# A two-layer gated network on one NeuronCore: a first layer in TensorE order written out by hand, side work in tables of slots, and every half of W2 multiplied from a split

## The chip, the cores and the metric

The program runs on one core of one Trainium2 chip. Its time is device time in microseconds (us), from the launch of the program to its end on that core. The kernel before was timed three times; the figure compared is the median. One further execution was taken with the hardware profiler.

## The reference

The input x has 4 batches of 512 tokens with 256 features, all in float32. The hidden width is 1024. Both layers have the same shape, `x = x + mix(xn) * silu(ffn(xn))` with `xn = layernorm(x)`; they differ in `mix`. Cut to what is computed:

```python
def ffn(x, W1, W3, W2):                      # W1, W3: 1024 x 256, W2: 256 x 1024
    hidden = silu(x @ W1.T) * (x @ W3.T)
    hidden = fwht(hidden)                    # Walsh-Hadamard over 1024, / sqrt(1024)
    return hidden @ W2.T

def mix0(x):                                 # one step of a recurrence from a zero state
    xi = (x @ W_in.T)                        # 512 channels, 16 states each
    y = sum(C_real * B_real * xi - C_imag * B_imag * xi, over the states)
    return x + rmsnorm(y @ W_out.T) * norm_w

def mix1(x):                                 # causal attention with one head of 256
    n = layernorm(x) * gamma + beta
    q, k, v = n @ qkv[:, :256], n @ qkv[:, 256:512], n @ qkv[:, 512:]
    return softmax(causal(q @ k.T / 16)) @ v @ o_proj + x

for mix, W1, W3, W2 in layers:
    xn = layernorm(x)
    x = x + mix(xn) * silu(ffn(xn, W1, W3, W2))
```

## The kernel before

**Precision.** A float32 operand is split into a part `hi`, a cast to the format fp32r that TensorE reads, and `lo = src - hi`. `split` does this with a cast on ACT (line 61) and a subtraction on DVE (line 62). `mm3` (line 80) then makes one product out of three of TensorE: hi by hi, lo by hi and hi by lo, added up in one PSUM bank. All TensorE instructions go through one helper, so that all have line 70 in the profile; they are told apart by their tiles.

**Weights.** The Walsh-Hadamard transform is moved from the hidden values to W2: `prep_w2` takes each half of W2 (128 of the 256 outputs, `w2raw`, 512 KB) through three butterfly stages on DVE (lines 155 and 156, tiles `w2b`) and then through a product with a 128 by 128 Hadamard matrix on TensorE (tile `w2ps`, two of 512 columns for a half), and splits the outcome into `w2h` and `w2l`. For half 0 of layer 0 that product is native: TensorE reads float32 on both sides (line 170). The other three halves are split first (`w2bh`, `w2bl`) and take two fp32r products for each 512 columns. `prep_m` folds W_in, the coefficients and W_out into one matrix m of 256 by 256 (tile `mps`). `prep_second` forms the products of the query and key weights and of the value and output weights, and `prep_s` forms sums of layer 1's weights, splits them and stores them to DRAM.

**First layer.** `ffn` works on one batch of 512 tokens in 8 chunks of 128 hidden features. A chunk has the gate and the up product (`gu`, three PSUM banks, 6 fp32r products of 512 columns for each of the two), silu on ACT (line 526, tile `h`), the gate product on DVE (line 527), the split of `h` into `hh` and `hl`, and the down products (`dn`, 12 of 256 columns). The down products of a chunk are issued `defer` = 1 chunks later, those of batch 0 all at the end. The trace calls the tiles of a batch f_0gu, f_1h and so on, and leaves the number of the layer or of the batch out where it can't tell them apart.

**Side work.** Beside the chunks go the mixer (`mixer`: 24 products of 256 columns, a copy `osb` and squares on ACT, a power on POOL, a scaling and an addition into `xn` on DVE, lines 730 and 733), the gate of the batch before (`gate`: silu on ACT, lines 702 and 704 on DVE, which give the new `x`), the layernorm and the transposes of the next batch (`norm`: statistics and scaling on DVE, a power on POOL, eight transposes on TensorE into the tiles `xt..tp0` and `tp1`, which are split into `xt`), and the preparation of weights. They are generators. The class `Beside` runs through them one after the other and spreads their steps evenly over 16 slots for each batch, two for each chunk: `slot(2 * c)` ahead of a down chunk and `slot(2 * c + 1)` behind it. Small PSUM results share three banks with the tag `ms`; the down products have two.

**Order of the engines.** Each engine's instructions are put in order when the program is built: the tile framework's scheduler places an instruction by its own model of time, as soon as that model says that its operands are there, and `issue_after` forces one instruction behind another. Queues are then worked through in order on the chip. `line["fixed"]` puts each TensorE instruction behind the one issued before it in the program; it is set at the end of layer 0, so that in layer 0 the scheduler chooses TensorE's order and in layer 1 the program does. DMAs go out from the SP queue, save half of the first load of x, which goes from ACT.

**Second layer.** `ffn_s` does the gate and up products with seven block products instead of eight, the attention's steps stand in tables (`places`) between them, and the order of TensorE is the program's.

Of the kernel before, what the change touches and what calls it, by code (L numbers as in the profile page):

```python
# [21 lines left out]
P = 128  # L22
D = 256
# [12 lines left out]
def kernel(ctx: ExitStack, tc: tile.TileContext, a: dict, out: bass.AP):  # L36
# [22 lines left out]
    def split(src, hi, lo, engine=nc.vector):  # L59

        h = nc.scalar.copy(hi, src)  # L61
        return h, engine.tensor_tensor(lo, src, hi.bitcast(F32), ALU.subtract)  # L62

# [13 lines left out]

    def mm3(o, terms, late=False):  # L80


        seq = [(l[0], r[0]) for l, r in terms]
        if late:
            seq += [(l[1], r[0]) for l, r in terms] + [(l[0], r[1]) for l, r in terms]
        else:
            for l, r in terms:
                seq += [(l[0], r[1]), (l[1], r[0])]
        for n, (l, r) in enumerate(seq):
            ins = matmul(o, l, r, start=n == 0, stop=n == len(seq) - 1)  # L90
        return ins
# [30 lines left out]
    def split_w13(layer, q, raw):  # L122
        both = wp.tile([P, 2, 2, S], F32R, tag="w13", name=f"w13_{layer}_{q}", bufs=4)
        hi, lo = both[:, 0], both[:, 1]
        if (layer, q) != (0, 0):
            split(raw, hi, lo)
            return hi, lo
        halves = [slice(c * D, (c + 1) * D) for c in range(2)]
        split(*(z[:, :, halves[0]] for z in (raw, hi, lo)))
        next(normed)  # L130
        with after(first["norm"][0]), after(first["norm"][1]):
            hi_, lo_ = split(*(z[:, :, halves[1]] for z in (raw, hi, lo)))
        first["w13"] = hi_, lo_
        return hi, lo
# [7 lines left out]

    def prep_w2(layer, raws, dst, scratch):

        w2h, w2l = dst
        for half in range(2):
            ds_ = slice(half * P, (half + 1) * P)
            cur = raws[half]  # L150
            for st, h in enumerate((1, 2, 4)):
                nxt = scratch(f"w2b{st}_{layer}_{half}", [P, NH, P])
                cv = cur.rearrange("p (g two h) d -> p g two (h d)", two=2, h=h)
                nv = nxt.rearrange("p (g two h) d -> p g two (h d)", two=2, h=h)
                nc.vector.tensor_tensor(nv[:, :, 0], cv[:, :, 0], cv[:, :, 1], ALU.add)
                nc.vector.tensor_tensor(nv[:, :, 1], cv[:, :, 0], cv[:, :, 1], ALU.subtract)
                cur = nxt
                yield

            native = layer == 0 and half == 0  # L160
            if not native:
                bh = t4(f"w2bh_{layer}_{half}", [P, NH, P], F32R)
                bl = t4(f"w2bl_{layer}_{half}", [P, NH, P], F32R)
                split(cur, bh, bl)
                yield
            for q in range(2):
                o = psum(f"w2ps_{layer}_{half}_{q}", [P, NH // 2, P])
                qs = slice(q * NH // 2, (q + 1) * NH // 2)
                if native:
                    matmul(o, had_f, cur[:, qs, :], start=True, stop=True)  # L170
                else:
                    matmul(o, had, bh[:, qs, :], start=True, stop=False)
                    matmul(o, had, bl[:, qs, :], start=False, stop=True)
                split(o, w2h[:, qs, ds_], w2l[:, qs, ds_])
                yield
# [14 lines left out]

    def prep_m(win, wout):

# [6 lines left out]
        wg = [t4(f"wg{i}", [P, 4, D], F32R) for i in "hl"]  # L199
        wi = [t4(f"wi{i}", [P, 4, D], F32R) for i in "hl"]  # L200
        for c in range(4):
# [4 lines left out]
            )  # L206
        split(win, *wi)
        yield
# [255 lines left out]

    def ffn(name, xT, w13, w2, slot, defer=1, spare=(), parts=1, behind=False, tail=()):

# [33 lines left out]
        for c in range(NH):  # L500
# [8 lines left out]
            for half in range(parts if c == 0 else 1):  # L509
                n = S // (parts if c == 0 else 1)  # L510
                ts_ = slice(half * n, (half + 1) * n)
                if parts == 1 or c:
                    for o, cols in gu:
                        last_up = mm3(o[:, ts_], k_pairs((wh, wl), cols, xT, ts_))
                    continue

                for n, (w, x) in enumerate(((wh, xT[0]), (wl, xT[0]), (wh, xT[1]))):
                    for o, cols in gu:
                        for k in range(2):
                            last_up = matmul(  # L520
                                o[:, ts_], w[:, k, cols], x[:, k, ts_],
                                start=n + k == 0, stop=n + k == 3,
                            )
            gu = [o for o, _ in gu]
            h = hid(f"{name}h{c}")
            first["silu"] = nc.scalar.activation(h, gu[0], AF.Silu)
            gates.append(nc.vector.tensor_tensor(h, h, gu[1], ALU.mult))  # L527
            first["gate"] = gates[-1]
# [184 lines left out]
    def mixer(b):  # L713
# [5 lines left out]
        for i in range(2):  # L719
            o = psum(f"o0_{b}_{i}", [P, 2, D])  # L720
            for j in range(2):
                mm3(o[:, j, :], k_pairs(xT, sl(2 * i + j), m, ALLD))
            nc.scalar.copy(osb[:, 2 * i : 2 * i + 2, :], o)
# [12 lines left out]
    class Attention:  # L736
# [45 lines left out]
        def tq(self, j):  # L782
# [3 lines left out]
            o = psum(f"tq{b}_{j}", [P, S])  # L786
            mm3(o, k_pairs(first["wqk"], sl(j), self.xg, ALLS), late=self.b > 0)
            split(o, self.tqs[0][:, j, :], self.tqs[1][:, j, :])
# [92 lines left out]
    class Beside:  # L881


        def __init__(self, *tasks, slots=2 * NH):
            self.slots = slots
            self.gens = [g for g, _ in tasks]
            self.total = sum(n for _, n in tasks)
            self.done = 0

        def step(self):  # L890
            while self.gens:
                try:
                    next(self.gens[0])
                    self.done += 1
                    return True
                except StopIteration:
                    self.gens.pop(0)
            return False

        def slot(self, k):  # L900
            if k + 1 >= self.slots:
                self.finish()
            while self.done < self.total * (k + 1) / self.slots and self.step():
                pass

        def finish(self):
            while self.step():
                pass

# [3 lines left out]
    def call(f, *args):  # L913
        f(*args)
        yield


    NORM, MIXER, W2P = 3, 3, 12

# [42 lines left out]
    def prep_first():  # L962
# [3 lines left out]
        yield  # L966
        for _ in range(4):
# [12 lines left out]
        next(product)  # L980
# [7 lines left out]
    def prep_second():  # L988
# [9 lines left out]
        yield  # L998


    dn = None
    for b in range(B):
        tasks = []
        if b == 0:
            prep = prep_first()
            next(prep)
            tasks.append((prep, 12))
        if b:
            tasks.append((call(gate_all, f"g0_{b - 1}", dn, xns[0, b - 1], xs[b - 1]), 1))
        tasks.append((mixer(b), MIXER))  # L1010
        if b + 1 < B:
            if b:
                load_x(b + 1)
            if b == 2:
                tasks.append((prep_s(0), 4))
            tasks.append((norm(0, b + 1), NORM))
        if b == 0:
            early = w2_tile("early0"), w2_tile("early1")
            spare = [
                [early[i][:, 2 * c : 2 * c + 2, :].rearrange("p a d -> p (a d)") for i in range(2)]  # L1020
                for c in range(NH // 2)
            ]
        if b == 1:
            raw2_1 = load_w2(1)
            w2_1 = w2_tiles(1)
            tasks.append((prep_w2(1, raw2_1, w2_1, t4), W2P))
            tasks.append((prep_second(), 5))
        if b == 2:
            tasks += [(prep_s(1), 4), (norm(1, 0), NORM), (prep_s(2), 4)]
        if b == 3:  # L1030
            atts = [Attention(0)]
            at = atts[0]
            parts = run(at.xt_half, 0), run(at.xt_half, 1), at.xt, at.scaled, at.split_sums
            tasks += [(call(f), 1) for f in parts]
            norms = {1: norm(1, 1)}
            tasks.append((prep_s(3), 4))
        bg = Beside(*tasks)
        if b == 0:
            dn = ffn("f0_0", xTs[0, 0], w13, w2, bg.slot, NH, spare, parts=2, behind=True)
        else:  # L1040
            tail = [run(atts[0].tq, j) for j in range(2)] if b + 1 == B else []
            dn = ffn(f"f0_{b}", xTs[0, b], w13, w2, bg.slot, tail=tail)
        bg.finish()

# [28 lines left out]

    line["fixed"] = True
    gate_all("g0_3", dn, xns[0, 3], xs[3])
    behind = None
    for b in range(B):
# [15 lines left out]
        if not final:  # L1093
            if b == 0:
                next(norms[1])
            places[0][2].append(run(next, norms[b + 1]))
# [95 lines left out]
```

## Time and profile before

| | us |
|---|---|
| median of 3 runs | 359.23 (359.09 to 359.24) |
| the profiled execution | 359.27 |
| its span in the profile | 357.5 |
| TensorE matmuls (PE) busy | 351.5 |
| weight loads (PEld) busy | 327.4 |
| VectorE (DVE) busy | 287.1 |
| ScalarE (ACT) busy | 197.6 |
| GpSimd (POOL) busy | 20.8 |

The span is the time from the first to the last instruction that the profiler saw; the 1.8 us between it and the execution's time lie around it. Busy times are sums over an engine's instructions; matmuls are pipelined, so that the busy time of one holds a part of the next. The clock that was granted to TensorE was 1.00. The DMA engines moved 52.25 MB, a mean of 146 GB/s. In the rows of a timeline the first column is the start, the second the duration of the group, then come the engine, the line, the operation, the tile written, the tiles read, the shapes and the count; in square brackets stand the idle time of the engine before the group and what ended it.

### The profile page before, as it was taken

Reading aid. Unit: us, or ns where it says so; the run is one execution under the profiler, and the core shown is the slowest. Engines: PE = TensorE matmul, PEld = TensorE weight load, DVE = VectorE, ACT = ScalarE, POOL = GpSimd, SP = SyncE. Lnnn points to the kernel's source line nnn. Section 1 sums busy time; section 2 is a strip of 40 time slices with the busy share of each in tenths; the row PEclk is TensorE's granted clock in tenths of the full one; section 3 lists DMA queues with packets and bytes.
Section 4 is the critical chain, followed back from the end, with each engine's and each line's share of the span. In section 5 each row is a group of like instructions: output and inputs, shape, how many; then the busy total and the mean of one; then the engine's idle time right before and its main releaser. Section 6 shows DMA issues by size and latency. Waiting matters only on the chain.

```text
span 357.5 us, 6272 instructions
## 1 busy us (share of the span) xinstructions
PE 351.5 (98%) x2477; PEld 327.4 (92%) x2477; DVE 287.1 (80%) x597; ACT 197.6 (55%) x373; POOL 20.8 (6%) x22
## 2 busy tenths in 40 slices
PE   8999999999999999999999999999999999999995
PEld 6878998888988898888999999999999999999995
DVE  6899648998579938898887957989679897568645
ACT  3666156256373424674367655576555676556443
POOL 2000110300020210100110001100011000000000
PEclk9999999999999999999999999999999999999999
DMA  7935000301044416656357145562554745345401
GB/s 222 357 95 202 2 1 2 92 25 61 0 151 160 163 27 219 256 177 198 129 208 254 27 191 207 205 224 105 205 193 150 230 169 205 142 150 192 194 2 59
DMA packets 16284, 52.25 MB, mean 146 GB/s; under 512 B 1632, under 2 KB 7936, under 8 KB 16256
## 3 DMA queue, kind: packets, MB, share of 16 engines
q1 hardware_dynamic: 15968, 51.60, 41.0%
q8 instruction: 19, 0.31, 0.4%
q10 hardware_dynamic: 288, 0.26, 0.2%
q14 instruction: 9, 0.07, 0.1%
HBM read 42.40 MB, written 9.45 MB: 145 GB/s over the span
## 4 chain that ended last, share of the span: by engine, by line
PE 98%; DVE 1%; ACT 0%; issue 0%; DVEq 0%
PE f_1dn L70 6%; PE f_2dn L70 6%; PE f_1gu L70 6%; PE f_0dn L70 6%; PE f_0gu L70 6%; PE f_2gu L70 6%; PE f_3gu L70 6%; PE f_3dn L70 6%; PE sc L70 4%; PE pv L70 4%; PE o L70 3%; PE v L70 3%; PE tq L70 3%; PE warm L70 2%; PE w2ps L70 1%; PE pt L70 1%
## 5 line engine op out<-in xcount | busy, mean ns | idle before, releaser
L70 PE MATMUL f_1gu<-xt,w 128*128 128x512 f32 x96 | 24.9, 396 | 0.3 <-ACT xt L61 0.3
L70 PE MATMUL f_3gu<-xt,w 128*128 128x512 f32 x96 | 25.0, 396 | 0.0
L70 PE MATMUL f_2gu<-xt,w 128*128 128x512 f32 x96 | 24.8, 395 | 0.0
L70 PE MATMUL f_0gu<-xt,w 128*128 128x512 f32 (+1 forms) x108 | 24.4, 379 | 0.0
L70 PEld LDWEIGHTS f_0gu<-xt,w 128*128 128x128 f32 x108 | 18.5, 188 | 4.5 <-issue 1.0
L70 PEld LDWEIGHTS f_1gu<-xt,w 128*128 128x128 f32 x96 | 17.0, 188 | 3.6 <-ACT xt L61 0.5
L70 PEld LDWEIGHTS f_2gu<-xt,w 128*128 128x128 f32 x96 | 17.0, 188 | 3.0
L70 PEld LDWEIGHTS f_3gu<-xt,w 128*128 128x128 f32 x96 | 17.0, 188 | 2.9
L61 ACT CAST f_2hh<-f_2h 128x512 fp32r<-128x512 f32 x16 | 10.0, 622 | 15.3 <-DVE f_2h L527 12.2
L70 PE MATMUL f_3dn<-w2l,f_3hh 128*128 128x256 f32 x64 | 17.7, 281 | 0.0
L70 PE MATMUL f_1dn<-w2l,f_1hh 128*128 128x256 f32 x64 | 17.7, 281 | 0.0
L70 PE MATMUL f_3dn<-w2h,f_3hh 128*128 128x256 f32 x64 | 17.7, 281 | 0.0
L70 PE MATMUL f_2dn<-w2h,f_2hh 128*128 128x256 f32 x64 | 17.7, 282 | 0.0
L70 PE MATMUL f_1dn<-w2h,f_1hh 128*128 128x256 f32 x64 | 17.6, 280 | 0.0
L70 PE MATMUL f_2dn<-w2l,f_2hh 128*128 128x256 f32 x64 | 17.6, 280 | 0.0
L70 PE MATMUL f_3dn<-w2h,f_3hl 128*128 128x256 f32 x64 | 17.0, 281 | 0.0
L70 PE MATMUL f_1dn<-w2h,f_1hl 128*128 128x256 f32 x64 | 17.0, 281 | 0.0
L70 PE MATMUL f_2dn<-w2h,f_2hl 128*128 128x256 f32 x64 | 16.7, 281 | 0.0
L61 ACT CAST f_3hh<-f_3h 128x512 fp32r<-128x512 f32 (+1 forms) x17 | 10.0, 594 | 10.2 <-DVE f_3h L527 6.0
L61 ACT CAST f_1hh<-f_1h 128x512 fp32r<-128x512 f32 x16 | 9.9, 622 | 9.7 <-DVE f_1h L527 6.6
L62 DVE TENSOR_TENSOR f_2hl<-f_2h,f_2hh 128x512 fp32r<-128x512 f32 x16 | 11.0, 686 | 4.5 <-ACT f_2hh L61 4.5
L62 DVE TENSOR_TENSOR f_3hl<-f_3h,f_3hh 128x512 fp32r<-128x512 f32 (+1 forms) x17 | 11.1, 655 | 3.7 <-ACT f_3hh L61 3.6
(487 smaller groups left out, 1149.0 us busy)
## 6 DMA issues: line engine op xcount, KB each, us to landing
sw<-s SPq DMA_DIRECT2D x32, 896.0 KB, 5.3
s<-sp SPq DMA_DIRECT2D x8, 512.0 KB, 4.6
s<-sp SPq DMA_DIRECT2D x8, 384.0 KB, 2.8
w2raw<-in_w SPq DMA_DIRECT2D x4, 512.0 KB, 5.4
sraw<-in_w SPq DMA_DIRECT2D x4, 512.0 KB, 3.3
mrb<-there SPq DMA_DIRECT2D x4, 512.0 KB, 3.7
w13raw<-in_w SPq DMA_DIRECT2D x3, 512.0 KB, 6.8
x<-in_x SPq DMA_DIRECT2D x3, 512.0 KB, 3.6
```

Of the source, the lines that this page charges most:

```text
L61: h = nc.scalar.copy(hi, src)
L62: return h, engine.tensor_tensor(lo, src, hi.bitcast(F32), ALU.subtract)
L70: ins = call(*args, **kwargs)
```

## The change

Six things are done at once.

1. **W2 all from splits.** Half 0 of layer 0 is split like the others and takes two fp32r products for each 512 columns; the native product is gone. `prep_w2` takes the halves that it is to do, so that the two halves of layer 1 become two generators.
2. **A split by DMA.** `split_by_dma` has ACT write the negated source to `lo` and the cast to `hi`, and has a DMA of the POOL queue add the source to `lo`. It is used for `w13_0_3`, the last quarter of layer 0's gate and up weights, behind the silu of chunk 2, and for `win`.
3. **Order in `mm3`.** The lo parts of one side come together, those of the left or of the right side last (`late`), instead of in turn.
4. **Down products two chunks later.** `defer` becomes 2, and the last down chunk of a batch is handed on (`pend`) and issued behind chunk 0 of the next batch's gate and up products.
5. **A fixed order.** `line["fixed"]` is set from batch 1 of layer 0 on.
6. **A table of slots.** `Beside` stays for batch 0 alone and takes a list of steps there. Batches 1 to 3 have a list of 16 slots each, with the steps of each slot written out. The gate has two steps now (silu, then the rest).

```diff
+    def split_by_dma(src, hi, lo):
+        nc.scalar.mul(lo, src, -1.0)
+        nc.scalar.copy(hi, src)
+        nc.gpsimd.dma_start(lo.bitcast(F32), src, accum_op=ALU.add)
...
-    def mm3(o, terms, late=False):
+    def mm3(o, terms, late=0):
         seq = [(l[0], r[0]) for l, r in terms]
-        if late:
-            seq += [(l[1], r[0]) for l, r in terms] + [(l[0], r[1]) for l, r in terms]
-        else:
-            for l, r in terms:
-                seq += [(l[0], r[1]), (l[1], r[0])]
+        for side in (1 - late, late):
+            seq += [(l[1 - side], r[side]) for l, r in terms]
...
-        if (layer, q) != (0, 0):
-            split(raw, hi, lo)
+        if q:
+            with after(first["silus"][2] if q == 3 else None):
+                (split_by_dma if q == 3 else split)(raw, hi, lo)
             return hi, lo
...
-            native = layer == 0 and half == 0
-            if not native:
-                bh = t4(f"w2bh_{layer}_{half}", [P, NH, P], F32R)
-                bl = t4(f"w2bl_{layer}_{half}", [P, NH, P], F32R)
-                split(cur, bh, bl)
-                yield
+            bh, bl = (t4(f"w2b{i}_{layer}_{half}", [P, NH, P], F32R) for i in "hl")
+            split(cur, bh, bl)
+            yield
...
-                if native:
-                    matmul(o, had_f, cur[:, qs, :], start=True, stop=True)
-                else:
-                    matmul(o, had, bh[:, qs, :], start=True, stop=False)
-                    matmul(o, had, bl[:, qs, :], start=False, stop=True)
+                matmul(o, had, bh[:, qs, :], start=True, stop=False)
+                matmul(o, had, bl[:, qs, :], start=False, stop=True)
...
-    def ffn(name, xT, w13, w2, slot, defer=1, spare=(), parts=1, behind=False, tail=()):
+    def ffn(name, xT, w13, w2, slot, defer=2, spare=(), parts=1, behind=False, tail=(), pend=()):
...
+            if c == 0:
+                for what in pend:
+                    what()
...
-        line["fixed"] = bool(tail)
-        line["last"] = last_up
+        left = [lambda q=q: down(*q) for q in queue]
+        if not behind:
+            left.pop(0)()
         for what in tail:
             what()
-        for q in queue:
-            down(*q)
-        return dn
+        if not behind and not tail:
+            return dn, left
+        for what in left:
+            what()
+        return dn, ()
...
     def prep_first():
...
-        for _ in range(2):
+        win, wout = raw_m
+        wi = [t4(f"wi{i}", [P, 4, D], F32R) for i in "hl"]
+        split_by_dma(win, *wi)
+        for _ in range(4):
             next(steps)
             yield
         load_x(1)
-        product = prep_m(*raw_m)
+        product = prep_m(wi, wout)
...
     for b in range(B):
+        if b:
+            line["fixed"] = True
+            g = gated(b - 1, dn)
+        m = mixer(b)
...
         if b == 0:
...
+            bg = Beside([prep] * 13 + [n] * 3 + [m] * 3, 16)
...
         if b == 1:
...
+            w, u = (prep_w2(1, raw2_1, w2_1, t4, (half,)) for half in range(2))
+            s = prep_second()
+            steps = [
+                [g, m, w], [m], [w, s], [w], [n], [w], [m], [u],
+                [u], [g], [w, w], [u, s], [n, n], [u], [s, s], [],
+            ]
         if b == 2:
...
+            o, p, q = (prep_s(i) for i in range(3))
+            r = norm(1, 0)
+            steps = [
+                [g, m, o], [m, u, u], [s, o], [n], [o], [m], [o, p], [g],
+                [p], [p], [r], [p, q], [n, n], [r], [q], [q],
+            ]
         if b == 3:
...
+            p = prep_s(3)
+            tail = [run(at.tq, j) for j in range(2)]
+            steps = [
+                [g, m, p, q], [m, r], [g], [h0], [h1], [x], [], [c],
+                [t], [p], [m], [p], [p], [], [norms[1]], [],
+            ]
+        dn, pend = ffn(f"f0_{b}", xTs[0, b], w13, w2, each(steps), tail=tail, pend=pend)
...
-    line["fixed"] = True
     gate_all("g0_3", dn, xns[0, 3], xs[3])
```

In the tables g is the gate of the batch before, m the mixer, n and r layernorms (of layer 0 and of layer 1), w and u the two halves of layer 1's W2, s `prep_second`, o, p and q `prep_s`, and h0, h1, x, c and t the first steps of layer 1's attention for batch 0.

More of the change, by code (lines that the diff above doesn't have):

```diff
@@ L141, in load_w2, with prep_w2 @@
         return raws
-    def prep_w2(layer, raws, dst, scratch):
+    def prep_w2(layer, raws, dst, scratch, halves=range(2)):
         w2h, w2l = dst
-        for half in range(2):
+        for half in halves:
             ds_ = slice(half * P, (half + 1) * P)
@@ L189, in load_m, with prep_m @@
         return win, wout
-    def prep_m(win, wout):
+    def prep_m(wi, wout):
         cb = wp.tile([P, 4, 2, DS], F32, name="cb")
@@ L199, in prep_m @@
         wg = [t4(f"wg{i}", [P, 4, D], F32R) for i in "hl"]
-        wi = [t4(f"wi{i}", [P, 4, D], F32R) for i in "hl"]
         for c in range(4):
@@ L206, in prep_m @@
             )
-        split(win, *wi)
         yield
@@ L513, in ffn @@
                     for o, cols in gu:
-                        last_up = mm3(o[:, ts_], k_pairs((wh, wl), cols, xT, ts_))
+                        last_up = mm3(o[:, ts_], k_pairs((wh, wl), cols, xT, ts_), late=int(not behind))
                     continue
@@ L526, in ffn @@
             first["silu"] = nc.scalar.activation(h, gu[0], AF.Silu)
+            first.setdefault("silus", []).append(first["silu"])
             gates.append(nc.vector.tensor_tensor(h, h, gu[1], ALU.mult))
@@ L721, in mixer @@
             for j in range(2):
-                mm3(o[:, j, :], k_pairs(xT, sl(2 * i + j), m, ALLD))
+                mm3(o[:, j, :], k_pairs(xT, sl(2 * i + j), m, ALLD), late=1)
             nc.scalar.copy(osb[:, 2 * i : 2 * i + 2, :], o)
@@ L786, in tq @@
             o = psum(f"tq{b}_{j}", [P, S])
-            mm3(o, k_pairs(first["wqk"], sl(j), self.xg, ALLS), late=self.b > 0)
+            mm3(o, k_pairs(first["wqk"], sl(j), self.xg, ALLS), late=1)
             split(o, self.tqs[0][:, j, :], self.tqs[1][:, j, :])
@@ L881, with __init__ @@
     class Beside:
[L884 to L898, printed above, removed]
+        def __init__(self, steps, total=0, slots=2 * NH):
+            self.steps, self.slots, self.done = steps, slots, 0
+            self.total = total or len(steps)
         def slot(self, k):
@@ L902, in slot @@
                 self.finish()
-            while self.done < self.total * (k + 1) / self.slots and self.step():
-                pass
+            while self.steps and self.done < self.total * (k + 1) / self.slots:
+                next(self.steps.pop(0))
+                self.done += 1
         def finish(self):
-            while self.step():
-                pass
+            while self.steps:
+                next(self.steps.pop(0))
     def run(f, *args):
@@ L915, in call @@
         yield
-    NORM, MIXER, W2P = 3, 3, 12
     load_x(0, 1, (nc.sync, nc.scalar))
@@ L966, in prep_first @@
         yield
-        for _ in range(4):
+        for _ in range(3):
             next(steps)
@@ L998, in prep_second, with gated, each, slot @@
         yield
-    dn = None
-    for b in range(B):
-        tasks = []
+    def gated(b, dn):
+        add = gate(f"g0_{b}", dn, xns[0, b], xs[b])
+        yield
+        add()
+        yield
+    def each(steps):
+        def slot(k):
+            for s in steps[k]:
+                next(s)
+        return slot
+    dn, pend = None, ()
+    for b in range(B):
+        if b:
+            line["fixed"] = True
+            g = gated(b - 1, dn)
+        m = mixer(b)
+        if b + 1 < B:
+            if b:
+                load_x(b + 1)
+            n = norm(0, b + 1)
         if b == 0:
@@ L1006 @@
             next(prep)
[L1007 to L1017, printed above, removed]
+            bg = Beside([prep] * 13 + [n] * 3 + [m] * 3, 16)
             early = w2_tile("early0"), w2_tile("early1")
@@ L1022 @@
             ]
+            dn, pend = ffn(
+                "f0_0", xTs[0, 0], w13, w2, bg.slot, NH, spare, parts=2, behind=True
+            )
+            continue
+        tail = ()
         if b == 1:
@@ L1025 @@
             w2_1 = w2_tiles(1)
-            tasks.append((prep_w2(1, raw2_1, w2_1, t4), W2P))
-            tasks.append((prep_second(), 5))
-        if b == 2:
-            tasks += [(prep_s(1), 4), (norm(1, 0), NORM), (prep_s(2), 4)]
+            w, u = (prep_w2(1, raw2_1, w2_1, t4, (half,)) for half in range(2))
[4 more added lines that the diff above has]
+            ]
+        if b == 2:
+            o, p, q = (prep_s(i) for i in range(3))
[4 more added lines that the diff above has]
+            ]
         if b == 3:
@@ L1032 @@
             at = atts[0]
-            parts = run(at.xt_half, 0), run(at.xt_half, 1), at.xt, at.scaled, at.split_sums
-            tasks += [(call(f), 1) for f in parts]
+            h0, h1, x, c, t = (
+                call(f)
+                for f in (run(at.xt_half, 0), run(at.xt_half, 1), at.xt, at.scaled, at.split_sums)
+            )
             norms = {1: norm(1, 1)}
[L1036 to L1043, printed above, removed]
+            p = prep_s(3)
[5 more added lines that the diff above has]
+        dn, pend = ffn(f"f0_{b}", xTs[0, b], w13, w2, each(steps), tail=tail, pend=pend)
     def store(b):
@@ L1093 @@
         if not final:
-            if b == 0:
-                next(norms[1])
             places[0][2].append(run(next, norms[b + 1]))
```

## The prediction, made before the changed kernel was run

> **What bounds the kernel now.** I read the page first, then the windows, then single engines in order of time.
>
> ```profile
> span 357.5 us, 6272 instructions
> PE 351.5 (98%) x2477; PEld 327.4 (92%) x2477; DVE 287.1 (80%) x597; ACT 197.6 (55%) x373; POOL 20.8 (6%) x22
> PE 98%; DVE 1%; ACT 0%; issue 0%; DVEq 0%
> ```
>
> TensorE is the chain. A busy PE need not be at its peak, so I look at starts:
>
> ```profile
> 17.86 1.02 PE L70 MATMUL w2ps<-w2b,had_f 128*128 128x512 f32 x2
> 18.32 1.97 PE L70 MATMUL f_0gu<-xt,w 128*128 128x512 f32 x6
> 20.13 1.02 PE L70 MATMUL w2ps<-w2b,had_f 128*128 128x512 f32 x2
> 29.86 1.56 PE L70 MATMUL f_0gu<-xt,w 128*128 128x512 f32 x6
> 31.25 0.64 PE L70 MATMUL mps<-wgh,wih 128*128 128x256 f32 x4
> 51.00 0.28 PE L70 MATMUL f_0dn<-w2h,f_0hl 128*128 128x256 f32 x1
> 51.60 0.73 PE L70 MATMUL f_1gu<-xt,w 128*128 128x512 f32 x2 [0.33 <-ACT xt L61]
> ```
>
> Six 512-column products take 1.39 us (29.86 to 31.25), 0.232 each; 256 columns take 0.118 by the same reading. From 8 us to the tail PE starts at this pace nearly everywhere. It loses time at two native W2 products (17.86 and 20.13; each shows as two records) and at one wait for xt (51.00 to 51.60 for a product worth 0.12). A gain must come from there; any new wait adds to the end. So who can make PE wait?
>
> ```profile
> core 0: us, PE busy (x) PEld busy (x) DVE busy (x) ACT busy (x) POOL busy (x), PEclk, DMA share, GB/s
> 54.00:85.00 31.00, 31.00 (x180) 27.01 (x179) 29.70 (x57) 16.61 (x32) 3.42 (x2) 1.00 0.16 52
> 95.00:131.00 36.00, 36.00 (x213) 31.61 (x212) 30.67 (x76) 17.14 (x35) 5.46 (x4) 1.00 0.32 118
> 131.00:172.00 41.00, 41.00 (x251) 36.41 (x251) 32.91 (x63) 22.39 (x44) 2.44 (x2) 1.00 0.64 211
> ```
>
> In batch 1 DVE is busy 29.70 of 31 us: PE is fed there with next to nothing to spare. What DVE did just before matters:
>
> ```profile
> 48.16 0.17 DVE L727 TENSOR_SCALAR ssr<-ssr 128x4 f32<-128x4 f32 x1 [5.19 <-ACT junk L725]
> 51.15 1.23 DVE L733 TENSOR_TENSOR xn<-xn,osb 128x1024 f32<-128x1024 f32 x1
> 53.49 1.28 DVE L702 TENSOR_TENSOR g_0g<-g_0g,xn 128x512 f32<-128x512 f32 x2
> 54.69 1.29 DVE L704 TENSOR_TENSOR x<-x,g_0g 128x512 f32<-128x512 f32 x2
> 56.97 0.69 DVE L527 TENSOR_TENSOR f_1h<-f_1h,f_1gu 128x512 f32<-128x512 f32 x1 [0.99 <-ACT f_1h L526]
> 64.65 0.66 DVE L527 TENSOR_TENSOR f_1h<-f_1h,f_1gu 128x512 f32<-128x512 f32 x1
> 66.43 1.67 DVE L730 SCALAR_TENSOR_TENSOR osb<-osb,ssr,nwb 128x256 f32<-128x256 f32 x4
> 68.01 0.69 DVE L155 TENSOR_TENSOR w2b<-w2raw 128x512 f32<-128x512 f32 x1
> 69.22 0.69 DVE L62 TENSOR_TENSOR f_1hl<-f_1h,f_1hh 128x512 fp32r<-128x512 f32 x1
> ```
>
> The mixer and gate of batch 0 (L730, L733, L702, L704) are done before batch 1's first gate product at 56.97, in time in which DVE had been waiting.
>
> **W2 all from splits.** Two native products go, four fp32r ones come. From 17.86 to 20.13 stand one native product and six others: 2.27 - 1.39 = 0.88 us; two fp32r cost 0.46. Saved: 2 x (0.88 - 0.46) = **-0.8**. In their place come, for that half, a cast on ACT (1.0) and a subtraction on DVE (1.14). The subtractions of w13_3 and win go from DVE to a GpSimd DMA that accumulates, behind a negated copy on ACT (about 1.0 each, by the 1024-column casts).
>
> ACT's built order after chunk 2's silu is: negate w13_3, cast it, cast w2bh. That silu ends at about 17.8 (PE 17.1 plus 0.6), so w2bh is there at 17.8 + 3.0 = 20.8. PE asks for it 10 products after 17.86, at 20.2: **+0.6** (0 to 1.0).
>
> w13_3's lo part is issued to the DMA at about 18.9, its consumer gu6 comes at 27.4. No accumulating DMA is in the trace. Nearest rows: 512 KB landed in 3.3 us (sraw) to 8.7 (win), that is 22.2 to 27.6; an accumulation moves more, so at the far end twice 8.7, 9 us late. I take 0: the 896 KB of sw<-s, nearest in traffic, landed in 5.3. win's lo stands behind it on POOL and is needed only after 32; POOL's next work, the pow of batch 1's norm, comes at about 40. [...]
>
> **PE in a fixed order from batch 1, orders of hi and lo, down products two chunks later.** Product counts stay; at equal pace, 0. Batch 1's transposes now stand 43 products ahead of their consumer (5 us), which hides the xt split: **-0.6** (both sides of 51.60). Without that cover it is 0.
>
> **What the fixed order moves onto DVE.** In the built order, batch 0's second mixer product is PE's last before batch 1's gu0, and the chunk-0 gate product stands in DVE's queue ahead of all mixer and gate work of batch 0. Queues are in order, so DVE idles until gu0 is through and then has 5.1 us more to do (1.58 + 1.13 + 1.20 + 1.20). Count from gu0's end.
>
> Prices, from start to start in DVE's rows of batch 1: a 512-wide operation 0.60 (57.58 to 58.18; a W2 stage is two), four scalings 1.58 (66.43 to 68.01), xn's add 1.13, four statistics 1.31 (61.19 to 62.50), a 1024-wide subtraction 1.14 (65.29 to 66.43). In the built order, DVE does: product h0 0.60, osb 1.58, W2 stage 1.20, hl0 0.60, xn 1.13, W2 1.20, sum 0.07, h1 0.60, gate 1.20, W2 1.20, osb 1.58, hl1 0.60, x 1.20, h2 0.60, stats 1.31, w2bl 1.14, W2 1.20, xn 1.13, aggregates 0.16, hl2 0.60: 18.9. With 0.26 for PE's drain and 0.15 for the result, hl2 is there at 19.3.
>
> PE until it needs hl2: 24 mixer products of 0.118, 2.83; gu1 to gu4, 4 x 12 x 0.233 = 11.2; two down chunks of 12 x 0.118, 2.83; two products 0.24: 17.1. **+2.2** (1.0 to 3.0). Behind the waiting product everything on PE waits.
>
> Next, the second transpose of batch 2 takes the bank that w2l of half 0 frees. DVE from hl2 to there: aggregates 0.16, h3 0.60, W2 1.20, 0.07, hl3 0.60, W2 1.20, h4 0.60, qk 1.13, xn 1.29, w2bl 1.14, hl4 0.60, vo 1.14, h5 0.60, w2l 0.60: 10.9. PE meanwhile: rest of down 1.18, gu5 2.80, w2ps 0.94, down 1.42, gu6 2.80, transposes 0.44: 9.6. **+1.4** (0 to 2.0).
>
> Batch 2 gets from batch 1 half of W2's end and wvo's split, 1.8 us of DVE, where 5.3 of 36 were free. Summed the same way, h4's product is there 27.3 us after gu0 (25.4 of work, 1.6 of waits for silu and w2h, 0.3 of latency); gu6 wants its bank at 26.3: **+1.1** (0 to 2.5). Batch 3 had 8 us of 41 free: 0 (up to 1.5). mrb now stands behind sw on SP, which waits for gu1; it lands about when DVE reaches it, and its consumers on PE are 5 us later. Layer 1's PE order is unchanged and had no gaps: delays pass straight through.
>
> **Sum:** -0.8 - 0.6 + 0.6 + 2.2 + 1.4 + 1.1 = +3.9, with 0.1 to 0.3 for DVE's late lo parts of batch 0: **+4.1**. The profiled execution took 359.27 (1.8 beside its span), the median is 359.23: **363.4**.
>
> A PE wait of 2 us raises the question of the clock. The granted clock is 1.00 in all windows, with no wait over 0.6 to test it; the first products, before PE had warmed, stood 0.427 apart instead of 0.232. [...]
>
> **Rivals.** (1) *Faster:* DVE's backlog doesn't bind, as two chunks' distance gives hl more time than my count. It decides if hl2 comes before 17.1 after gu0, that is if DVE does 2.2 of the 18.9 us elsewhere, or faster. Then only -0.8 - 0.6 + 0.6 are left: 358.4. For it: DVE had idle time ahead of batch 1. Against: the built queue puts the work behind a product that can't start there. Chance 0.15. (2) *No change:* DVE's stalls are half as long and are paid by what is won: about 359.2 to 359.9. Chance 0.05. (3) *Late DMA:* w13_3's lo lands after 27.4; priced at a landing of 11 us, 2.5 late: 366. For it: nothing like it in the trace. Chance 0.07. (4) *Clock or more waits:* 1.5 to 3 more, in batch 2 and 3: 365 to 367. Chance 0.07. The forecast itself: 0.66, own range 360.8 to 365.5.
>
> Low end 359.2: under it lies rival 1. High end 366.5: above it lie the far DMA bound and the end of rival 4, about 0.05. Faster by over 0.2% (0.7 us, what a measurement here can tell) 0.15, same 0.05, slower 0.80.
>
> **What would show it.** Right: DVE without idle time from batch 1's first gate product for some 30 us; PE idle before f_1dn<-w2h,f_1hl of chunk 2 (ended by DVE L62) and before the batch-2 transposes (ended by DVE w2l); w2ps in batch 0 waits for ACT w2bh; no native rows and no wait at 51. Wrong: PE at pace through batch 1, or idle before gu6 of batch 0, ended by a DMA.

## The result and the profile after

The changed kernel takes 364.15 us (median of 4 runs, 364.13 to 364.37) against 359.24 before: a ratio of 1.0139, with a 95% interval from 1.0127 to 1.0151. It is 4.9 us slower; the forecast was 4.2 slower, at 363.4. The profiled execution took 364.37 with a span of 362.6.

The page of the changed kernel, with the lines that answer to those of before:

```profile
span 362.6 us, 6280 instructions
PE 352.2 (97%) x2477; PEld 326.6 (90%) x2477; DVE 286.1 (79%) x596; ACT 200.1 (55%) x376; POOL 22.0 (6%) x24
PE 77%; DVE 14%; ACT 3%; DMA 2%; issue 1%; SPq 1%; DVEq 0%
```

Work has hardly changed: PE is busy 0.7 us more, DVE 1.0 less. The chain has: 14% of it is now DVE. (Line numbers have moved: the matmul helper is L76 here.) The table of PE's waits says where (engine, tile, what it waited for, then the sum in us, the number of waits and the longest). These are its rows behind the start:

```profile
PE f_1dn L76 <- DVE f_1hl L62: 2.0, 1, 2.0
PE xt_2tp L76 <- DVE w2l L62: 1.1, 1, 1.1
PE f_2gu L76 <- DVE f_2h L527: 0.5, 1, 0.5
PE w2ps L76 <- ACT w2bh L61: 0.2, 1, 0.2
PE f_2gu L76 <- ACT f_2h L525: 0.2, 1, 0.2
```

The kernel before has none of these five waits; three of them are on DVE. (Two more stand at the start, 0.4 and 0.2 long; the first gate product comes 0.17 later than before.) The product behind a wait is itself followed some 0.1 us late, which I call a restart. So I count from start to start and take off the pace of 0.118 and 0.233: 2.31 with the hl of chunk 2, 1.31 at the second transpose for batch 2, 1.5 around the last third of batch 2 (0.63 and 0.37 at the two waits, and five restarts of 0.1), 0.5 at the first W2 product. Two rows of PE's timeline show what went in exchange, the native products and the wait for xt:

```profile
20.83 0.73 PE L76 MATMUL w2ps<-w2bh,had 128*128 128x512 f32 x2 [0.23 <-ACT w2bh L61]
51.34 2.96 PE L76 MATMUL f_1gu<-xt,w 128*128 128x512 f32 x12
```

Batch 1 starts at 51.34 instead of 51.60, and its first products follow each other without a wait. PE stands 0.27 us ahead there, and 5.0 behind where layer 1's score products begin (180.7 against 175.7). So all of the loss lies in batches 1 and 2 of layer 0, and layer 1 passes it on unchanged. What DVE did around the start of batch 1:

```profile
46.83 1.29 DVE L62 TENSOR_TENSOR xt<-xt_1tp,xt 128x512 fp32r<-128x512 f32 x2 [3.50 <-ACT xt L61]
53.24 0.17 DVE L730 TENSOR_SCALAR ssr<-ssr 128x4 f32<-128x4 f32 x1 [5.12 <-ACT junk L728]
54.41 0.69 DVE L527 TENSOR_TENSOR f_1h<-f_1h,f_1gu 128x512 f32<-128x512 f32 x1 [1.00 <-PE f_1gu L76]
55.01 1.67 DVE L733 SCALAR_TENSOR_TENSOR osb<-osb,ssr,nwb 128x256 f32<-128x256 f32 x4
...
58.40 1.22 DVE L736 TENSOR_TENSOR xn<-xn,osb 128x1024 f32<-128x1024 f32 x1
...
66.00 1.28 DVE L707 TENSOR_TENSOR x<-x,g_0g 128x512 f32<-128x512 f32 x2
...
72.75 0.66 DVE L62 TENSOR_TENSOR f_1hl<-f_1h,f_1hh 128x512 fp32r<-128x512 f32 x1
```

DVE stands idle for 5.1 us up to 53.24, waiting for the squares of batch 0's mixer (`junk`), and does the scaling, xn's addition and the gate of batch 0 between batch 1's chunks. Before, `ssr` came at 48.16 and all of that was over by 56. The hl of chunk 2 now comes at 72.75, where PE had waited since 71.4. From 54 to 90 DVE was busy for 34.23 of 36.00 us (after the length of the stretch come PE, weight loads, DVE, ACT and POOL, then the granted clock):

```profile
54.00:90.00 36.00, 32.87 (x190) 28.33 (x189) 34.23 (x63) 16.85 (x32) 4.09 (x3) 1.00 0.05 15
```

### The profile page after: what moved, and what is told of

It reads as the page before. It is cut to its first block, busy times and chain, and to the rows that moved or that the text cites. A ratio compares the mean times of both kernels' runs of the same rounds, so it can differ in the third digit from the quotient of the medians.

```text
span 362.6 us, 6280 instructions
## 1 busy us (share of the span) xinstructions
PE 352.2 (97%) x2477; PEld 326.6 (90%) x2477; DVE 286.1 (79%) x596; ACT 200.1 (55%) x376; POOL 22.0 (6%) x24
## 3 DMA queue, kind: packets, MB, share of 16 engines
q1 hardware_dynamic: 15968, 51.60, 39.9%
q0 software_dynamic: 288, 1.05, 1.8%
## 4 chain that ended last, share of the span: by engine, by line
PE 77%; DVE 14%; ACT 3%; DMA 2%; issue 1%; SPq 1%; DVEq 0%
PE f_0dn L76 6%; PE f_3gu L76 6%; PE f_3dn L76 6%; PE f_1dn L76 5%; PE f_2dn L76 5%; PE sc L76 4%; PE pv L76 4%; PE v L76 3%; PE tq L76 3%; PE f_0gu L76 3%; DMA w13raw<-in_w 2%; PE f_2gu L76 2%; PE o L76 2%; PE f_1gu L76 2%; DVE osb L733 1%
## 5 line engine op out<-in xcount | busy, mean ns | idle before, releaser
L76 PE MATMUL f_2gu<-xt,w 128*128 128x512 f32 x96 | 24.2, 398 | 0.7 <-DVE f_2h L527 0.5
L76 PE MATMUL f_3gu<-xt,w 128*128 128x512 f32 x96 | 23.8, 396 | 0.0
L76 PE MATMUL f_0gu<-xt,w 128*128 128x512 f32 (+1 forms) x108 | 23.6, 371 | 0.2 <-ACT xt L414 0.2
L76 PE MATMUL f_1gu<-xt,w 128*128 128x512 f32 x96 | 23.5, 395 | 0.0
L76 PEld LDWEIGHTS f_0gu<-xt,w 128*128 128x128 f32 x108 | 18.3, 188 | 4.3 <-ACT xt L414 0.4
L76 PEld LDWEIGHTS f_2gu<-xt,w 128*128 128x128 f32 x96 | 17.3, 188 | 5.2 <-ACT f_2h L525 0.9
L76 PEld LDWEIGHTS f_1gu<-xt,w 128*128 128x128 f32 x96 | 17.5, 188 | 3.7
L76 PEld LDWEIGHTS f_3gu<-xt,w 128*128 128x128 f32 x96 | 17.4, 188 | 3.6
L76 PE MATMUL f_1dn<-w2h,f_1hl 128*128 128x256 f32 x64 | 18.0, 282 | 2.0 <-DVE f_1hl L62 2.0
L76 PE MATMUL f_3dn<-w2h,f_3hh 128*128 128x256 f32 x64 | 18.1, 283 | 0.0
L76 PE MATMUL f_1dn<-w2h,f_1hh 128*128 128x256 f32 x64 | 18.1, 282 | 0.0
L76 PE MATMUL f_2dn<-w2h,f_2hh 128*128 128x256 f32 x64 | 18.1, 282 | 0.0
L76 PE MATMUL f_1dn<-w2l,f_1hh 128*128 128x256 f32 x64 | 18.0, 282 | 0.0
L76 PE MATMUL f_3dn<-w2l,f_3hh 128*128 128x256 f32 x64 | 18.0, 282 | 0.0
L76 PE MATMUL f_2dn<-w2h,f_2hl 128*128 128x256 f32 x64 | 18.0, 281 | 0.0
L76 PE MATMUL f_2dn<-w2l,f_2hh 128*128 128x256 f32 x64 | 18.0, 281 | 0.0
L76 PE MATMUL f_3dn<-w2h,f_3hl 128*128 128x256 f32 x64 | 17.9, 280 | 0.0
L76 PEld LDWEIGHTS f_1dn<-w2h,f_1hl 128*128 128x128 f32 x64 | 12.1, 189 | 2.2 <-DVE f_1hl L62 2.2
```

Source lines behind the costliest of these rows:

```text
L76: ins = call(*args, **kwargs)
```

## The experiments

All figures are medians. Runs 1 to 4 were made on one chip, 5 to 8 on a second and 9 to 12 on a third, each group with the kernel before beside it: 359.17, 359.23 and 359.21. These differ by 0.06, so that I compare times across the groups as they stand.

**1. The mixer of batch 0 before the norm of batch 1.**

```diff
-            bg = Beside([prep] * 13 + [n] * 3 + [m] * 3, 16)
+            bg = Beside([prep] * 13 + [m] * 3 + [n] * 3, 16)
```

> Only the order of batch 0's last side steps goes back: mixer before norm. Then the built DVE order has batch 0's scalings, xn's addition and both gate steps (5.1 us) ahead of batch 1's first gate product. Theory (the late mixer pushes 5.1 us of DVE work into batch 1): hl2 comes 14.2 us after gu0, before the 17.1 at which PE asks; the 2.3 us there and nearly all of the 1.3 us before batch 2's second transpose go, batch 2's own 1.5 us stay: 364.15 - 3.6 = 360.5 (360.2 to 361.2), and no new wait for xt of batch 1, as the transposes still stand 35 products ahead. Rival (the slot table of batch 1 or the fixed order overloads DVE whatever comes before it): above 363.

Measured: 360.61 (ratio to before 1.0039, 1.0024 to 1.0054). DVE's timeline of this kernel:

```profile
43.65 0.17 DVE L730 TENSOR_SCALAR ssr<-ssr 128x4 f32<-128x4 f32 x1 [0.24 <-ACT junk L728]
44.94 1.67 DVE L733 SCALAR_TENSOR_TENSOR osb<-osb,ssr,nwb 128x256 f32<-128x256 f32 x4 [1.12 <-POOL ssr L731]
...
52.50 1.29 DVE L707 TENSOR_TENSOR x<-x,g_0g 128x512 f32<-128x512 f32 x2
54.13 0.69 DVE L527 TENSOR_TENSOR f_1h<-f_1h,f_1gu 128x512 f32<-128x512 f32 x1 [0.35 <-PE f_1gu L76]
...
69.57 0.65 DVE L62 TENSOR_TENSOR f_1hl<-f_1h,f_1hh 128x512 fp32r<-128x512 f32 x1
```

The time that the theory gave (360.5) came out. One line of the change carries 3.5 us. `ssr` comes 9.6 us earlier, the mixer and gate work is done before the first gate product, and both waits of batch 1 are gone; those of batch 2 are as they were (0.63 and 0.42). Hl of chunk 2 comes 15.4 us after the gate product of chunk 0 instead of 18.3.

**2. The native product kept.**

```diff
+            native = layer == 0 and half == 0
+            if not native:
-            split(cur, bh, bl)
-            yield
+                split(cur, bh, bl)
+                yield
...
+                if native:
+                    matmul(o, had_f, cur[:, qs, :], start=True, stop=True)
```

> Half 0 of layer 0's W2 goes back to the native product, without its split. Theory: two natives cost 0.83 more than the four fp32r products, the wait for the w2bh cast (0.5 with its restart) goes: 364.15 + 0.3 = 364.5 (364.0 to 365.0), and batch 1's waits stay as they are. Rival (the split's cast and subtraction are what makes batch 0 late): under 363.7.

Measured: 366.55 (1.021, 1.0195 to 1.0225), outside what either theory gave. It is not the price of the native product alone: the built order put both natives together at 17.8, and PE then waited 1.7 us for a bank that ACT's silu frees. In the profiled execution, the longest at 367.46, TensorE also ran at half pace for a while after the wait of 2.0 in batch 1. A table by stretches (columns as above):

```profile
73.40:76.80 3.40, 1.37 (x8) 1.02 (x8) 3.40 (x9) 0.00 (x0) 0.00 (x0) 1.00 0.00 0
76.80:80.20 3.40, 3.40 (x14) 3.01 (x13) 3.40 (x8) 2.11 (x4) 1.81 (x1) 0.50 0.00 0
80.20:83.60 3.40, 3.40 (x19) 2.86 (x18) 3.40 (x7) 3.40 (x6) 0.77 (x1) 1.00 0.00 0
```

In the middle row the clock is 0.50, the products stand 0.213 and 0.427 apart, and TensorE takes 1.6 us longer there; the wait for the bank of batch 2's transposes, 1.31 in the changed kernel, is then missing. The half pace does not make the median: the two executions with a clock of 1.00 took 366.50 and 366.60. Batch 1 starts at 54.23 instead of 51.34, so that the loss of 2.4 comes from batch 0. The other order there covers what the experiment was made for, and the natives' price rests on the rows of the traces.

**3. No accumulating DMA.**

```diff
-                (split_by_dma if q == 3 else split)(raw, hi, lo)
+                split(raw, hi, lo)
...
-        split_by_dma(win, *wi)
+        split(win, *wi)
```

> w13_0_3 and win are split by a cast and a DVE subtraction, without the accumulating DMA. ACT gets rid of two negations of 0.95, DVE gets two subtractions of 1.14 in batch 0, and the built order puts half of batch 0's mixer behind the start of batch 1. Theory: the wait for w2bh shrinks by 0.4, the mixer is as late or later for DVE: 364.3 (363.6 to 366). Rival (the accumulating DMA holds something up): under 363.

Measured: 365.36, with executions from 364.62 to 366.52 (1.0165, 1.0145 to 1.0184): within the range, but for other reasons than given. The wait for the first half's w2bh did go; the second half's w2bh then came late, as its butterflies stood behind the two subtractions on DVE. By their mean granted clock (0.993 and 0.995, against 0.992 in run 2's profile) the two longest, the profiled execution among them, have the half pace as well and the two others (0.998) do not; these took 364.62 and 364.75, 0.5 more than the changed kernel. Run 11 repeats this where PE has no wait of 2 us.

**4. TensorE's order fixed from layer 1 on only.**

```diff
         if b:
-            line["fixed"] = True
             g = gated(b - 1, dn)
...
+    line["fixed"] = True
     gate_all("g0_3", dn, xns[0, 3], xs[3])
```

> TensorE's order is fixed from layer 1 on only, as in the kernel before; all else as changed. Built, the down products come in pieces of 4 and 8 between the gate and up products, DVE's order still has batch 0's mixer and gate work behind batch 1's first gate product. Theory: the same backlog makes PE wait: 363.5 (362 to 365.5). Rival (the fixed order itself makes the waits): under 361.

Measured: 360.70 (1.0041, 1.0026 to 1.0056). The rival was right: the theory, 363.5, missed by 2.8. DVE is as late as in the changed kernel (`ssr` at 52.90, hl of chunk 2 at 72.41), but PE's timeline shows other work in front of the late product:

```profile
70.22 1.56 PE L76 MATMUL f_1gu<-xt,w 128*128 128x512 f32 x6
71.62 0.63 PE L76 MATMUL w2ps<-w2bl,had 128*128 128x512 f32 x2
73.12 0.39 PE L76 MATMUL f_1dn<-w2h,f_1hl 128*128 128x256 f32 x1 [0.87 <-DVE f_1hl L62]
```

The W2 products and a gate product come first, the down products in pieces, and 0.87 is left of the wait. The one for the transpose's bank is gone; a wait for the gate product of a chunk (0.45 with its restart) has come into batch 1, and batch 2 keeps 0.3.

**5. Both orders back.** Edits 1 and 4 together.

> Both changes of order together go back: mixer before norm in batch 0, and TensorE's order fixed from layer 1 on only. Theory (the waits of batch 1 need both a late DVE and an order in which PE can't do other work): the two waits of 1.1 and 0.45 that the free order kept in batch 1 go, 0.3 in batch 2 stays: 360.70 - 1.6 = 359.1 (358.7 to 359.6). Rival (the free order has a cost of its own, in its pieces of down products): 360 or more.

Measured: 358.72 (0.9985, 0.9975 to 0.9994). After the start, PE's table has one wait, the 0.2 for w2bh. From here, the fixed order alone costs 1.89 (run 1, 360.61), the late mixer alone 1.98 (run 4, 360.70), and both 5.43 (364.15): 1.56 more than their sum.

**6. Fixed order, early mixer, and batch 2 relieved.** Edit 1, and the middle of the weight sums held behind later gate products, the last part moved to batch 3:

```diff
+    def held(g):
+        while True:
+            with after(first["gate"]):
+                try:
+                    next(g)
+                except StopIteration:
+                    return
+            yield
...
+            p, q = held(p), held(q)
...
                 [g, m, o], [m, u, u], [s, o], [n], [o], [m], [o, p], [g],
-                [p], [p], [r], [p, q], [n, n], [r], [q], [q],
+                [p], [r], [p], [], [n, n, p], [r], [], [q],
...
-                [g, m, p, q], [m, r], [g], [h0], [h1], [x], [], [c],
+                [g, m], [m, r], [g, q], [h0], [h1, q], [x], [q, p], [c],
```

> Mixer before norm in batch 0, order fixed. In batch 2 the sums and splits of the second part of layer 1's weights (1.35 + 0.87 + 1.14 of DVE) are held behind the gate products h4 and h5, and the third part goes to batch 3. Theory (batch 2's two waits of 0.74 and 0.53, hesitations included, are DVE reaching h3 and h4 late, by work that stands ahead of them): both go, with four hesitations of 0.1: 360.61 - 1.5 = 359.1 (358.8 to 359.8). Rival (the work is only moved on, batch 3 has no room for it): 360.2 or more, with a wait in batch 3.

Measured: 359.06 (0.9994, 0.9984 to 1.0004). Batch 2's waits are gone and none came in batch 3: 1.55 us won, 1.5 expected. The fixed order costs little where DVE is in time: 359.06 here against 358.72 in run 5, which has the free order and the weight sums in their old place.

**7. The same, with ACT's cast of w2bh earlier**, ahead of the cast of w13_0_3, which now stands behind the silu of chunk 3.

```diff
+    def split_by_dma(src, hi, lo, behind=None):
         nc.scalar.mul(lo, src, -1.0)
-        nc.scalar.copy(hi, src)
         nc.gpsimd.dma_start(lo.bitcast(F32), src, accum_op=ALU.add)
+        with after(behind):
+            nc.scalar.copy(hi, src)
...
-                (split_by_dma if q == 3 else split)(raw, hi, lo)
+                if q == 3:
+                    split_by_dma(raw, hi, lo, first["silus"][3])
+                else:
+                    split(raw, hi, lo)
```

> As the run before, and ACT casts w2bh ahead of the hi part of w13_0_3, which comes behind silu of chunk 3; the accumulating DMA is issued right behind the negation, as before. Theory: w2bh is there 0.95 sooner, the wait of 0.5 at the first W2 product goes: 358.6 (358.3 to 359.2), faster than the kernel before by 0.6. Rival (PE then waits for the next thing in batch 0, the split's lo part or the silu): 359.0 or more.

Measured: 358.89 (0.999, 0.9981 to 1.0000). W2 no longer waits, but `mps` waits 0.33 for ACT's scaled W_out (0.5 with its restart): the rival, in part.

**8. The kernel before, with W2 all from splits alone.** The counts of the preparation's steps grow by the one that the split adds.

```diff
-            native = layer == 0 and half == 0
+            native = False
...
```

> The kernel before with one change: half 0 of layer 0's W2 is split and takes fp32r products. Its built ACT order has w2bh right behind silu of chunk 2, so that w2bh is there at about 18.8, before PE asks. Theory: 0.83 won by the natives, the wait for xt of batch 1 stays or grows by 0.3, as the built order has only five products between the last transpose and the first that needs xt: 359.2 - 0.5 = 358.7 (358.3 to 359.6). Rival (DVE's extra subtraction of 1.14 makes the lo parts of batch 0 late): 359.6 or more.

Measured: 359.90, with executions from 359.52 to 360.53 (1.0022, 1.0012 to 1.0031). The time of the rival: alone, this part loses 0.7. The 0.83 of the natives is won, and batch 0 pays 1.5 for it, at waits that the kernel before hasn't: 0.8 around the second half's W2 product, where a bank waits for DVE's gate product, 0.5 at `mps`, 0.2 behind it.

**9. The best of these.** Edits 1, 4 and 7, and the mixer's coefficients made earlier (three small DVE operations, of which the last was done at 29.05 in run 7 and kept ACT from scaling W_out before 29.14):

```diff
         nc.vector.tensor_reduce(g, cbd, AX.X, ALU.add)
+        yield
...
-        for _ in range(4):
+        product = prep_m(wi, wout)
+        for i in range(4):
+            if i == 1:
+                next(product)
             next(steps)
             yield
...
```

> Mixer before norm, order fixed from layer 1 on only, ACT's cast of w2bh ahead of the hi part of w13_0_3, and the coefficients of the mixer's matrix (three small DVE operations) made while the second half of W2 is in its butterflies, so that ACT's scaling of W_out starts as soon as it is free. Theory (batch 0 is left with the wait for w2bh and nothing behind it): 358.72 - 0.5 = 358.2 (357.9 to 358.6). Rival (PE only meets the next late operand of batch 0, as it met ACT's scaled W_out in the run with the cast moved): 358.6 or more.

Measured: 358.55 over 11 runs, ten of them between 358.41 and 358.81 and one at 360.00 (0.9984, 0.9975 to 0.9993). That is 0.7 us faster than the kernel before. The waits of PE after its first product:

```profile
PE xt_0tp L77 <- DVE xn L404: 0.4, 1, 0.4
PE f_1gu L77 <- ACT xt L61: 0.3, 1, 0.3
```

The wait for w2bh and the one for W_out are gone, and the old wait for xt is back, since the order that was built now leaves too little between the transposes and batch 1. Of 0.5 expected 0.2 arrived.

**10. Down products one chunk later instead of two.** Edits 1 and 6, and:

```diff
-    def ffn(name, xT, w13, w2, slot, defer=2, ...
+    def ffn(name, xT, w13, w2, slot, defer=1, ...
```

> Mixer before norm and batch 2's weight sums held, order fixed, and the down products one chunk later instead of two. Theory (DVE's queue of batch 1 needs the second chunk of distance): summed over the built DVE order, hl1 comes 10.4 us and hl2 15.4 us after gu0, PE asks at 10.1 and 14.6: 359.06 + 1.1 = 360.1 (359.4 to 361.5). Rival (the distance is worth nothing once the mixer is early): 359.3 or less.

Measured: 367.91 (1.0241, 1.0227 to 1.0255). The sign was right, the size far off: 8.9 us more than in run 6 instead of 1.1. PE waits for hl in all three batches:

```profile
PE f_2dn L76 <- DVE f_2hl L62: 2.8, 3, 2.3
PE f_1dn L76 <- DVE f_1hl L62: 1.7, 2, 1.2
PE f_3dn L76 <- DVE f_3hl L62: 1.1, 2, 0.9
```

These are the waits of the table; from start to start the down products lose 2.3, 4.4 and 2.1 us in batches 1, 2 and 3, together 8.7 of the 8.9. I had counted batch 1's DVE queue, at half of what it costs (1.1), and not those of batches 2 and 3. The second chunk is what makes a fixed order bearable.

**11. Edits 1 and 6, without the accumulating DMA** (edit 3).

> Mixer before norm and batch 2's weight sums held, order fixed, and w13_0_3 and win split with DVE's subtraction instead of the accumulating DMA. Theory (DVE is short of time in batch 0 too, and the DMA takes 2.3 us off it): the waits that the run without the DMA showed in batch 0 come back, 2.4 us instead of 0.8: 359.06 + 1.6 = 360.7 (359.8 to 361.5). Rival (the DMA split is worth nothing, as the subtractions hide): 359.3 or less.

Measured: 360.83 (1.0046, 1.0031 to 1.0061), 1.77 more than run 6. PE waits 1.15 for the second half's w2bh, with its restart, and 0.57 behind it, nearly as in run 3, and 0.8 for xt of batch 1. So the accumulating DMA is worth 1.8 us here: not by its own length, but as it takes 2.3 us from DVE ahead of the butterflies.

**12. The changed kernel once more**, for the clock.

> The changed kernel once more, unaltered, for the clock. Two runs had TensorE at half pace for 3.4 us after a wait of 2.3 us, the changed kernel's profile had the same wait and no loss. [...] If it is the length of the wait alone: all executions within 0.3 of 364.2.

Measured: 364.23, with executions at 363.89, 364.20, 364.25 and 364.60. None took the 1.6 more of run 2's stretch at half pace, but 363.89 and 364.60 lie outside the 0.3 expected. The mean granted clocks are 1.000, 0.993, 1.000 and 0.992: by these, two had the half pace, and it cost them little. The last section goes into this.

## Why the prediction was right

**Point by point.** In brackets the forecast.

- Native products: four fp32r products of 0.233 stand where 1.76 stood, -0.83 (-0.8).
- The wait for w2bh: +0.5 (+0.6). w2bh was ready at 20.8 (20.8).
- The accumulating DMA for w13_3: 0 (0). It was issued at 19.20 and landed 5.4 later, at 24.6, ahead of chunk 6, whose products start at 26.5 (27.4 in the forecast):

```profile
w<-w13raw POOLq DMA_DIRECT2D x1, 512.0 KB, 5.4
wil<-win POOLq DMA_DIRECT2D x1, 512.0 KB, 5.7
```

 The rows of the trace before, 3.3 to 8.7, had the measured 5.4 between them. That an accumulation moves more, as the forecast's far end assumed, was not shown: the page counts 1.05 MB for the two DMAs of 512 KB.
- The wait for xt of batch 1: -0.6 (-0.6).
- Hl of chunk 2: +2.31 (+2.2). The bank for batch 2's second transpose: +1.31 (+1.4). Batch 2, h3's and h4's gate products and the silu: +1.5 (+1.1).
- Beside these, +0.2 at the start, where the first gate product came at 8.05 instead of 7.88 (waiting for ACT's first xt), and some 0.4 of restarts in batch 0, of 0.1 each, at products whose operand came just in time.

The sum forecast was +4.1, the span grew by 5.1, the median by 4.9. The term most off is batch 2, +0.4: two waits were counted as one, without the restarts. Restarts were left out throughout.

**What the prediction had wrong though its sum was right.** It headed the largest term "What the fixed order moves onto DVE", and said that DVE idles because the gate product of chunk 0 stands ahead of the mixer's work in its queue. Run 1, the rows of DVE and one of POOL show another reason, which the prediction had seen on PE but not followed up (the mixer's second product is PE's last before batch 1): in batch 0, where the order is not fixed at all, the mixer's steps come behind those of the norm, PE does their products last, and their squares and the power on POOL are through only at 54.5, a tenth after the gate product could start:

```profile
53.49 1.01 POOL L731 TENSOR_TENSOR ssr<-ssr,mhalf 128x4 f32<-128x4 f32 x1 [11.57 <-DVE ssr L730]
```

The queue's order then hardly mattered; the operands weren't there. That the two came within a tenth of each other, so that counting from the end of chunk 0's products gave the right wait all the same, was luck. What the fixed order does is the second half: run 4 has the same late DVE and loses 3.5 us less, since PE does something else meanwhile. "Product counts stay; at equal pace, 0" was too short for the part on orders: the second chunk of distance is worth 8.9 us in the fixed order (run 10), and without it the change would have been far worse. The order within `mm3` was not tried by itself.

**The rivals.** Faster, if DVE did 2.2 us of the queue elsewhere: run 1 does 5.1 elsewhere, and the waits of batch 1 go, but batch 2's stay and it ends at 360.61, not at the 358.4 given for it. That rival lacked a term of its own for batch 2. Late DMA: no. The clock: not in the first four executions of the changed kernel (mean granted clock 0.999 to 1.000), but by their mean clock in two of the four of run 12 (0.993 and 0.992), which were some 0.2 longer than the changed kernel's others and not the 1.5 or more of the rival. No row of the kernel before showed that 1.5; the nearest measured is the 1.6 of run 2's stretch at half pace.

## What to carry to other kernels

An order written out by hand fixes not only what an engine does but what it may not do meanwhile: before fixing TensorE's order, sum up the queue of the engine that feeds it, from the first operand that is there, batch by batch, and give the consumer as much distance as that sum. A step put last in a list is late for everything behind it in the other engines' queues, also where it takes the producing engine no time more (3.5 us here, by run 1). An engine busy for 95% of a stage (DVE here, 34.23 of 36.00 us) has no room for work that comes late, even if it stood idle for as long just before (5.1 us here).

## What the runs showed of the hardware

TensorE idled for 2.0 to 2.3 us at one place in batch 1 or 2 of five profiles: 2.0 in run 2, 2.2 in run 3, 2.0 in both profiles of the changed kernel and 2.3 in run 10. In run 2 the granted clock behind that wait was 0.50 from 76.80 to 80.20, with 1.00 in the stretches before and after (the table there), and its mean over the execution was 0.992. In run 3's profile the mean was 0.993. In both profiles of the changed kernel and in run 10's it was 1.000. So the length of the wait alone doesn't tell the two cases apart: 2.0 stands on both sides, and the longest, 2.3, on the side of the full clock. What does was not shown.

The executions that were not kept as traces have their mean granted clock on record. It is 0.997 or more in every execution of a kernel without a wait of 2 us. A stretch of 3.4 us at 0.50, as in run 2, takes 0.005 off the mean over its span of 365.7 us (an estimate). By this, 8 of the 20 executions of the four kernels with such a wait had such a stretch: two of four in runs 2, 3 and 10 each (0.992 to 0.995), and two of the eight of the changed kernel (0.992 and 0.993); the other 12 stand at 0.998 or more. What it costs differs: in the mean 0.2 us in the changed kernel, 0.4 in runs 2 and 10, 1.6 in run 3. In the profiles of runs 2 and 3 the wait for the bank of batch 2's transposes, 1.1 in the changed kernel's table, is missing. So TensorE may lose at half pace what it would otherwise have waited for DVE a little later; this is not shown, and why run 3 pays in full stays open.
